# One batched attention and convolution kernel on one core: the v rows of its second pass loaded in two pieces that do not overlap

## The chip, the cores and the metric

The kernel runs on one core of a Trainium2 chip. The time is the device time of one launch in microseconds. Before the change it is 3721.15 us, the median of three runs (3717.85 to 3721.29). The profile is of one further execution, with a time of its own.

## The reference

The input x is a batch of 8 images of 256 channels and 64 x 64 pixels, in float32. Two layers follow each other. The first is an attention with keys and values from a 4 x 4 strided convolution. The second, which the change concerns, makes q, k and v by a 1 x 1 convolution, runs a depthwise 5 x 5 convolution over all three, mixes the result in groups of eight channels, and uses both the plain and the convolved set for a linear attention:

```python
qkv = jnp.einsum('oc,bchw->bohw', w_qkv, x)
dw = jax.lax.conv_general_dilated(qkv, w_dw, window_strides=(1, 1), padding=[(2, 2), (2, 2)], ...)
agg = jnp.einsum('goi,bgihw->bgohw', w_pw, dw.reshape(B, G, I, H, W)).reshape(B, G * O, H, W)
ms = jnp.concatenate([qkv, agg], axis=1)
...
kv = jnp.einsum('bhnd,bhne->bhde', k, v)
out = jnp.einsum('bhnd,bhde->bhne', q, kv)
out = out[..., :-1] / (out[..., -1:] + ATT_EPS)
```

Here n runs over the 4096 pixels, q and k are passed through a ReLU, and v has a column of ones added.

## The kernel before

The kernel has three passes, and keeps what one leaves for the next in scratch tensors in device memory. The first pass (`first_pass`) runs the first layer and the 1 x 1 convolution of the second. It writes q and k as planes (`planes`), k once more as tokens (`kd`), and v as tokens (`vd`). Image b has in `vd[b]` eight blocks, one for each 32 channels. A block is a grid of 34 x 34 tokens of 128 floats, 512 bytes each: a token holds a 2 x 2 cell of pixels with 32 channels, and the outermost tokens are a border of zeros (`border`).

The second pass (`second_pass`, from line 1121) makes the sums over pixels of k times v, for the plain and for the convolved set, and the convolved q. It works through 64 units, `(t, k, b)`: two halves of the channels, four blocks in each, eight images. For unit u it

- loads kq and vq (`load_tokens`, lines 1162 to 1176), the planes d1 and d0 that the convolutions of k and q need (`load_cells`, line 1158), and for each new (t, k) the convolution weights w (`load_weights`, line 1152);
- makes the differences c of neighbouring cells (`paired`, lines 1185 to 1189, on VectorE and GpSimd);
- convolves k on TensorE (`convolve`, line 1244), finishes it as s on VectorE (line 1260) and r on ScalarE (line 1262);
- sums plain k times v (`summed_raw`, line 1277), after a ReLU of kq on ScalarE (`positive`, line 1227);
- sums convolved k times v (`summed`, line 1294), a unit later. This uses that a convolution of v against k is a sum over shifted v: each partition needs its tokens and their neighbours;
- convolves q (line 1248, then s and r in lines 1260 and 1264), two units later, and stores it (`stored`, line 1343), with the small stores kv (line 1326) and kvg (line 1336).

For vq a partition has four rows of six tokens. The 128 partitions are 16 pairs of token rows times eight groups of four columns. A partition reads the two rows of its own and two further ones, and in each the four columns of its group and the two that follow, which are also the first two of the next group. The load is one transfer for each of the four rows, with a source that steps by four tokens and reads six: its rows of 3072 bytes overlap by 1024 (lines 1173 to 1175). vq has three buffers in turn, kq, d1 and d0 two each.

`summed_raw` reads rows 1 and 2 of vq and tokens 1 to 4; `summed` reads all of vq.

The third pass (`third_pass`) divides by the sums, projects, adds and writes the output. Its first loads and products (`ahead`) are called for in the last five units of the second pass: raw (line 1449, with a ReLU in line 1538), the sums kvp and kvq (lines 1491 and 1493), agg (line 1465).

All transfers are issued by SyncE, in one queue, in the order that the scheduler of the framework gives them; it orders each engine's instructions by its own estimates, save where `tc.keep_in_program_order` holds them. A transfer waits for its buffer to come free, and for its landing semaphore: there are eight, used in turn, so a transfer waits until the one eight before it has landed.

Of the kernel before, what the change touches and what calls it, by code (L numbers as in the profile page):

```python
# [32 lines left out]
P = 128  # L33
# [4 lines left out]
NB = HH // R  # L38
# [1082 lines left out]
def second_pass(ctx: ExitStack, tc: tile.TileContext, a, planes, kd, vd, wtd, kvd, kvg, qd, ahead):  # L1121
    nc = tc.nc
# [39 lines left out]
    def load_tokens(u):  # L1162
        t, k, b = units[u]
        kq = (odd if u % 2 else first).tile([P, 2, 4, P], F32, tag=f"kq_{u % 2}", name=f"kq_{u}")
        nc.sync.dma_start(
            kq.rearrange("p a c e -> p a (c e)"),
            kd[b][4 * t + k].rearrange("a y (m i) b e -> (y m) a (i b e)", i=2),
        )
        kqs[u] = kq
        vq = (first, odd, second)[u % 3].tile([P, 4, 6 * P], F32, tag=f"vq_{u % 3}", name=f"vq_{u}")  # L1170
        v = vd[b][4 * t + k]
        row = (NB2 + 2) * P
        for r in range(4):
            src = [[2 * row, NB], [4 * P, NB // 2], [1, 6 * P]]
            nc.sync.dma_start(vq[:, r], bass.AP(tensor=v.tensor, offset=v.offset + r * row, ap=src))
        vqs[u] = vq.rearrange("p r (c f h e) -> p r c f h e", c=6, f=4, h=4)


# [13 lines left out]
    for g in range(4):  # L1192
        load_weights(0, 1, g)
    load_cells(0, 1)
    load_tokens(0)
    load_cells(1, 1)
    load_tokens(1)
    def load(home, src, name):
        t = home.tile(list(src.shape), F32, tag=name, name=name)
# [150 lines left out]
    for u in range(n_all + 3):  # L1350
        p, q, r = u - 1, u - 2, u - 3
# [5 lines left out]
        if 1 < u < n_all - 1:  # L1357
            load_tokens(u + 1)
# [511 lines left out]
```

## Time and profile before

| | us |
|---|---|
| median of three runs | 3721.15 |
| the profiled execution | 3723.3 |
| its span, first to last instruction | 3721.5 |
| TensorE busy | 3655.3 |
| VectorE busy | 2050.1 |
| ScalarE busy | 1348.7 |
| GpSimd busy | 1362.7 |
| TensorE line 1244 (convolution of k) | 376.9 |
| TensorE line 1294 (sums over vq) | 308.6 |
| TensorE clock granted, share of full | 0.991 |

The page of the profile gives busy time, not useful time: matmuls are pipelined, and the record of a matmul can hold some waiting. The busy tenths cut the span in 40 slices of 93 us; the second pass fills those from about the 22nd to the 33rd. A transfer is listed by tile and source, with its kilobytes. The DMA share is the time that packets took, over that of 16 engines.

### The profile page before, as it was taken

The numbers are of one execution on the slowest core, as the hardware profiler recorded it, in microseconds if no ns is written. First come the engines' busy times: TensorE is split into PE (matmuls) and PEld (weight loads), VectorE is DVE, ScalarE is ACT, GpSimd is POOL, SyncE is SP. The second block draws the span as 40 slices with busy tenths as digits, with TensorE's granted clock in tenths as the row PEclk, the third lists the DMA queues.
The fourth block names the chain that finished last, engine by engine and source line by source line (L and its number), as shares of the span: only waits on it lengthen the run. The fifth ranks groups of instructions, "written<-read, shape, count | busy, mean of one in ns | idle before, by whom it ended". The sixth has DMA issues, their size and how long they took to land.

```text
span 3721.5 us, 65545 instructions
## 1 busy us (share of the span) xinstructions
PE 3655.3 (98%) x25506; PEld 2021.3 (54%) x25506; DVE 2050.1 (55%) x3159; ACT 1348.7 (36%) x2761; POOL 1362.7 (37%) x1394
## 2 busy tenths in 40 slices
PE   8999999999999999999998999999999999999998
PEld 4443534435334344353336888888888884333333
DVE  1567576675766755746675544444444445445442
ACT  2344354443443534434542222322222223333322
POOL 2434343343443433434443333433334321222222
PEclk9999999999999999999999999999999998999999
DMA  5336456464464553543648999999989968778773
GB/s 180 103 104 188 130 143 179 129 190 145 123 206 120 150 156 106 145 124 96 176 111 234 265 275 273 252 248 263 266 242 261 240 187 234 224 216 238 226 213 102
DMA packets 557071, 693.98 MB, mean 186 GB/s; under 512 B 79952, under 2 KB 416336, under 8 KB 556752
## 3 DMA queue, kind: packets, MB, share of 16 engines
q1 hardware_dynamic: 556752, 689.70, 66.2%
q8 instruction: 203, 3.33, 0.4%
q14 instruction: 116, 0.95, 0.1%
HBM read 415.15 MB, written 274.40 MB: 185 GB/s over the span
## 4 chain that ended last, share of the span: by engine, by line
PE 94%; DMA 2%; DVE 1%; ACT 1%; issue 1%; SPq 1%; POOL 0%; POOLq 0%; ACTq 0%; DVEq 0%
PE qkv L917 16%; PE p L1593 12%; PE cv L1244 9%; PE cv L1248 9%; PE sc L795 7%; PE sums L1294 7%; PE av L819 6%; PE o L873 6%; PE q L780 6%; PE sr L707 6%; PE den L839 3%; PE rep L1579 2%; PE den L1560 1%; PE raw L1277 1%; DMA wsr<-in_w_sr_dram 1%
## 5 line engine op out<-in xcount | busy, mean ns | idle before, releaser
L832 POOL TENSOR_TENSOR ej<-e,e 128x512 f32<-128x512 f32 x512 | 679.2, 1355 | 957.8 <-ACT e L801 957.8
L801 ACT ACTIVATE e<-sc 128x512 f32<-128x512 f32 x1024 | 529.9, 608 | 581.9 <-PE sc L795 581.9
L1244 PE MATMUL cv<-w,c 128*128 128x128 f32 x3072 | 376.9, 280 | 7.3 <-DVE eps L1615 6.2
L1260 DVE TENSOR_TENSOR s<-cv,both 128x512 f32<-128x512 f32 x256 | 176.6, 691 | 374.5 <-PE cv L1244 192.4
L1244 PEld LDWEIGHTS cv<-w,c 128*128 128x128 f32 x3072 | 354.8, 192 | 37.5 <-issue 36.4
L1603 POOL TENSOR_TENSOR y<-z,xs 128x512 f32<-128x512 f32 x128 | 165.7, 1302 | 458.6 <-ACT z L1601 427.0
L1294 PE MATMUL sums<-vq,r 128*32 128x288 f32 x4096 | 308.6, 414 | 0.2 <-issue 0.2
L795 PE MATMUL sc<-q,kk 32*128 32x512 f32 x2048 | 299.6, 639 | 0.0
L917 PE MATMUL qkv<-differences,combined 128*128 128x512 f32 x576 | 291.3, 597 | 0.5 <-POOL differences L890 0.5
L1593 PE MATMUL p<-raw,wp 128*128 128x512 f32 x512 | 246.9, 604 | 5.2 <-ACT z L1601 5.1
L819 PE MATMUL av<-e,vv 128*32 128x512 f32 x2048 | 248.3, 598 | 0.6 <-ACT e L801 0.6
L707 PE MATMUL sr<-x,wsr 128*128 128x256 f32 x1024 | 235.3, 384 | 9.1 <-DMA wsr<-in_w_sr_dram 9.1
L780 PE MATMUL q<-x,wq 128*128 128x512 f32 x512 | 241.9, 594 | 0.0
L1593 PE MATMUL p<-agg,wp 128*128 128x512 f32 x512 | 240.4, 592 | 0.0
L1248 PE MATMUL cv<-c,w 128*128 128x128 f32 x2048 | 239.1, 275 | 0.0
L1248 PEld LDWEIGHTS cv<-c,w 128*128 128x128 f32 x2048 | 234.3, 192 | 0.0
L873 PE MATMUL o<-att,wout 128*128 128x512 f32 x512 | 231.2, 593 | 0.0
L1251 ACT COPY both<-cv 128x512 f32<-128x512 f32 x128 | 74.9, 585 | 429.1 <-PE cv L1244 370.1
L707 PEld LDWEIGHTS sr<-x,wsr 128*128 128x128 f32 x1024 | 195.8, 192 | 63.8 <-issue 26.2
L852 DVE STREAM_TRANSPOSE rden<-den 128x512 f32<-128x512 f32 x128 | 90.9, 710 | 216.7 <-PE den L839 211.8
L788 ACT COPY q<-q 128x512 f32<-128x512 f32 x128 | 75.1, 586 | 371.7 <-PE q L780 371.7
L933 DVE TENSOR_TENSOR whole<-part,qkv 128x512 f32<-128x512 f32 x256 | 172.6, 684 | 67.2 <-ACT part L979 47.3
(143 smaller groups left out, 5277.2 us busy)
## 6 DMA issues: line engine op xcount, KB each, us to landing
vq<-v SPq DMA_DIRECT2D x256, 384.0 KB
planes<-stage SPq DMA_DIRECT2D x128, 578.0 KB
d<-planes SPq DMA_DIRECT2D x128, 578.0 KB
raw<-planes SPq DMA_DIRECT2D x64, 578.0 KB
x<-in_xp_dram SPq DMA_DIRECT2D x64, 512.0 KB
wsr<-in_w_sr_dram SPq DMA_DIRECT2D x128, 256.0 KB
x<-x SPq DMA_DIRECT2D x128, 256.0 KB
k<-turned SPq DMA_DIRECT2D x256, 128.0 KB
```

The source lines that it names most:

```text
L707: nc.tensor.matmul(ps[:, oc], w[:, ci, oc * P : (oc + 1) * P], strips(b, f // 2)[:, ci, f % 2 * NK : (f % 2 + 1) * NK], start=(f == ci == ...
L780: nc.tensor.matmul(ps, consts["wq"][:, ci, c * P : (c + 1) * P], strips(b, s)[:, ci], start=(ci == 0), stop=(ci == 1),)
L795: nc.tensor.matmul(scs[h], kks[b][rows, c, kc * P : (kc + 1) * P], qs[rows], start=True, stop=True)
L801: nc.scalar.activation(e, scs[h], AF.Exp, scale=D0**-0.5)
L819: nc.tensor.matmul(sums["av"][cols], vvs[b][:, kc, c * P + h * D0 : c * P + (h + 1) * D0], es[h], start=(kc == 0), stop=(kc == 1),)
L832: nc.gpsimd.tensor_tensor(e, es0[h], es1[h], ALU.add)
L873: nc.tensor.matmul(ps, consts["wout"][:, c, oc * P : (oc + 1) * P], att[c], start=(c == 0), stop=(c == 1))
L917: nc.tensor.matmul(ps, w, x, start=True, stop=True)
L1244: nc.tensor.matmul(out, x, m, start=(da == 0), stop=(da == 1))
L1248: nc.tensor.matmul(out, m, x, start=(da == 0), stop=(da == 1))
L1294: nc.tensor.matmul(ps[h * D0 : (h + 1) * D0, : 36 * D1].rearrange("p (r n e) -> p r n e", r=3, e=D1), kt[:, par, h, 2 * r + c], vq[:, r : ...
L1593: nc.tensor.matmul(as_block(ps, i // 2), wp[:, i, oc * P : (oc + 1) * P], block(g, i // 2, i % 2, j), start=(i == 0), stop=(i == 3),)
```

## The change

Each of the four rows of vq is loaded by two transfers instead of one: the four tokens of the partition's own group (2048 bytes), and the two tokens that follow (1024 bytes), into the same places of the same tile. First come the four rows' own tokens, then the four rows' two further ones. A unit so has eight vq transfers instead of four, of 256 and 128 KB instead of 384; the bytes that are read stay the same. No transfer names an address twice.

```diff
         row = (NB2 + 2) * P
-        for r in range(4):
-            src = [[2 * row, NB], [4 * P, NB // 2], [1, 6 * P]]
-            nc.sync.dma_start(vq[:, r], bass.AP(tensor=v.tensor, offset=v.offset + r * row, ap=src))
+        own = 4 * P
+        for c0, n in ((0, own), (own, 2 * P)):
+            for r in range(4):
+                src = [[2 * row, NB], [own, NB // 2], [1, n]]
+                nc.sync.dma_start(
+                    vq[:, r, c0 : c0 + n], bass.AP(tensor=v.tensor, offset=v.offset + r * row + c0, ap=src)
+                )
         vqs[u] = vq.rearrange("p r (c f h e) -> p r c f h e", c=6, f=4, h=4)
```

The scheduler then places some instructions of the second pass otherwise, in both ends of it: on VectorE the c of unit 6 comes after the s of unit 5 instead of before, on ScalarE the r of unit 55 before the second ReLU of raw, and on SyncE the second half of the first raw load after d, kv and kvg.

## The prediction

> **What bounds the kernel now.** I read the page first: its head, the busy tenths, the queues and the transfers.
>
> ```profile
> span 3721.5 us, 65545 instructions
> PE 3655.3 (98%) x25506; PEld 2021.3 (54%) x25506; DVE 2050.1 (55%) x3159; ACT 1348.7 (36%) x2761; POOL 1362.7 (37%) x1394
> PE   8999999999999999999998999999999999999998
> DMA  5336456464464553543648999999989968778773
> ...
> vq<-v SPq DMA_DIRECT2D x256, 384.0 KB
> ```
>
> TensorE is busy for 98%. All that it leaves idle is 3721.5 - 3655.3 = 66 us, and no cheaper transfer can bring more than the part of it that waits for transfers. But in the middle of the DMA row, where the second pass is, the engines stand at 9: nearly full. The changed transfer, vq, moves 256 x 384 KB, 1.57 MB in each of 64 units.
>
> Next I took windows. Columns: window, length, busy time of PE, PEld, DVE, ACT and POOL, TensorE clock, DMA share, GB/s.
>
> ```profile
> 2505.00:2506.00 1.00, 1.00 (x12) 1.00 (x11) 0.47 (x3) 0.10 (x1) 0.00 (x0) 1.00 0.65 236
> 2507.00:2512.00 5.00, 5.00 (x46) 5.00 (x45) 2.88 (x7) 1.38 (x3) 1.63 (x2) 1.00 1.05 242
> 2514.00:2515.00 1.00, 1.00 (x12) 1.00 (x11) 0.36 (x1) 0.60 (x2) 0.13 (x1) 1.00 1.00 391
> 2519.50:2522.00 2.50, 2.50 (x28) 1.93 (x21) 2.34 (x6) 0.00 (x0) 0.00 (x0) 1.00 0.53 142
> 2040.00:2240.00 200.00, 195.82 (x2683) 167.11 (x2683) 96.09 (x178) 54.96 (x81) 77.73 (x85) 0.99 1.01 270
> 2300.00:2900.00 600.00, 600.00 (x8298) 519.94 (x8297) 286.52 (x543) 172.50 (x254) 239.22 (x254) 1.00 0.93 255
> ```
>
> One packet's time is 16 engines x bytes x share / rate. The second window holds vq alone, in rows of 3072 bytes: 16 x 3072 x 1.05 / 242 = 213 ns. The third holds weight rows (w) of the same 3072 bytes: 126 ns. So vq is read at some 60% of the rate that the same row has elsewhere. The first window is kq, rows of 2048 bytes: 90 ns; the fourth is q, rows of 1024 bytes: 61 ns. The last two rows give the stage: at the start of the pass transfers are full (1.01) and TensorE misses 4.2 us of 200; from 2300 to 2900 they are at 0.93 and TensorE misses nothing.
>
> Who TensorE waits for, from 2000 to 2940 us:
>
> ```profile
> PE few L1330 <- POOL red_agg L1222: 4.0, 1, 4.0
> PE raw L1277 <- ACT kq L1227: 2.8, 1, 2.8
> PE cv L1244 <- issue: 1.1, 1, 1.1
> PE sums L1294 <- issue: 0.2, 1, 0.2
> ```
>
> The first is the ramp of the pass, with no transfer behind it. The second has one, seen on VectorE and ScalarE:
>
> ```profile
> 2110.63 0.73 DVE L1185 TENSOR_TENSOR c<-d 128x544 f32<-128x544 f32 x1 [5.72 <-DMA d<-planes]
> 2111.27 0.72 DVE L1186 TENSOR_TENSOR c<-d 128x544 f32<-128x544 f32 x1
> 2111.91 1.28 DVE L1260 TENSOR_TENSOR s<-cv,both 128x512 f32<-128x512 f32 x2
> ```
>
> VectorE waits 5.72 us for a d tile, with s queued behind it, and s leads over r to kq and to TensorE's raw. Last, SyncE's queue in one unit of the steady stage:
>
> ```profile
> 2503.48 0.54 SPq L1165 DMA_DIRECT2D kq<-k  x1
> 2504.12 2.48 SPq L1175 DMA_DIRECT2D vq<-v  x4
> 2509.64 0.81 SPq L1152 DMA_DIRECT2D w<-wt  x2
> 2511.82 0.37 SPq L1158 DMA_DIRECT2D d<-planes  x1
> ```
>
> Four vq issues take 2.48 us, 0.62 each, and 5.2 us pass between the last of them (2506.6) and the next d, which waits for TensorE to leave its buffer.
>
> [...] kq, vq, w and d follow each other in the windows as they were issued, so a slow vq delays the d behind it. [...] the trace's rows (90 ns for 2048 bytes, 61 for 1024, 126 for 3072) agree that cutting a row costs a little.
>
> **The change part by part.**
>
> *Bytes and packets.* The same 3072 bytes per partition and row now come as 2048 and 1024. Before, the two steady windows that I took of vq alone gave 213 ns and, at 2524 to 2529 us, 16 x 3072 x 0.99 / 253 = 192; I take 200. A unit has 4 x 128 rows on 16 engines, 32 per engine: 32 x 200 = 6.4 us. After, if overlap was the cause: 32 x (90 + 61) = 4.8 us; saved 1.6 us per unit. If it was not, and the time goes by bytes, 6.4 again. If each packet paid the surplus over the w row (200 - 126 = 74 ns) for itself, 32 x (90 + 74 + 61 + 74) = 9.6 us, 3.2 more. I take the first: kq also has neighbouring rows of neighbouring partitions, but touching and not overlapping, and is fast, and w has rows far apart and is fast. Overlap is what vq alone has. The ends -1.6 and +3.2 us per unit stay for the range.
>
> *Steady stage.* TensorE misses nothing there, so saved transfer time is worth nothing. What hides a loss: 0.93 of a 16.6 us unit is 15.4 us of transfers, 1.2 us free. A vq is also issued early: the one at 2504 us is for unit 33, used by raw at 2532.7 us, 29 us after its kq was issued (12 to 20 us in the first units); landed by about 2515, it has some 17 us in hand.
>
> *SyncE's queue.* Eight issues in place of four: + 4 x 0.62 = 2.5 us per unit, in front of w, d, kv, kvg and the q stores. The 5.2 us before d cover it: the last vq issue moves to 2509.1, w to 2510.3, d stays at 2511.8. The program gives its transfers eight landing semaphores in turn, each waiting for the transfer eight before; eight shorter transfers are fewer bytes in flight, but at 4.8 us of data against 5 us of issue the queue is not starved. Cost 0. In the first pass the two early loads (1834 to 1843 us) take 5 us more of a queue that stands idle until 1847.8 us: 0 to 0.3 us, on stores that nobody waits for there.
>
> *Order.* The scheduler moves things. VectorE gets s of unit 5 ahead of c of unit 6, the pair of the 2110 us stall: its 2.8 us go even if transfers stay slow. With vq 1.6 us shorter in each of the first units, the d loads come earlier, and the 1.1 and 0.2 us go too: -4.2 us. At the start of the third pass, ScalarE waits 4.92 us for the load of raw, and TensorE 3.53 us at 2951.75 us for the kq behind it. That load stands behind vq: the four more issues delay it 2.5 us (2940.65 to 2943.1), the faster vq leaves the engines free just then; two changes that cancel, 0 +- 1.5 us. The next stall (3.02 us at 3024) hangs on 14 small transfers after q, and those of 3092 on the new pass's loads; no vq stands in them: 0.
>
> *Sum.* The profiled execution took 3723.3 us, 1.8 us around its span. 3723.3 - 4.2 = 3719.1. The median of the runs (3721.15) lies 2.15 us under the profiled one, so the median after is 3717.0. A measurement of this kernel can tell about 0.2%, 7.4 us, from no change: this would not be told.
>
> **The rivals.**
>
> *Rates stay, only the order moves.* For it: no price is known for overlap, and vq's rate wanders (213 and 192 ns) as it would if the placing of v in memory slowed it. Then the start stays full; -2.8 us from the order, up to +3 from the longer queue: 3721.
>
> *Slower: each of the two packets pays the surplus.* In the steady stage transfers would need 15.4 + 3.2 = 18.6 us of 16.6, and become the bound. It decides from about 1.5 us more per unit (1.2 free, and 17 us in hand over some 57 units), that is vq above 7.9 us, 247 ns per row. Price: 57 x 2.0 - 17 = 97 us, 3818. Against it: kq and q rows show no such surplus. A part of it (a halo that is slow alone, +1.6 us) would still be just hidden or cost some 10 to 20 us, 3735.
>
> *Slower: SyncE too late.* If landing waits stretch the eight issues by more than the 2.7 us left before d, d, kv and q come late, then c, and TensorE at cv: up to 0.3 us in each of 57 units, 3738. Against it: from 2300 to 2900 the queue waits on a landed vq for 1.8 us in all.
>
> *Faster still.* The stall at 2951 us goes as well, as ScalarE's order there also changes (r before the second raw): another -3.5 us, 3713.5.
>
> **How the numbers follow.** Forecast 0.55; rates stay 0.17; faster still 0.11; full surplus 0.06; partial surplus or a late SyncE 0.11. The forecast's own range is 3713 to 3721. From 3710 to 3732 all but the full surplus, half of the partial cases and a small tail are held, some 0.85. Faster by over 0.2% (under 3713.7): half of the last rival and a tail of the forecast, 0.14. Slower (over 3728.6): 0.06 + 0.11 and 0.01, 0.18. Between: 0.68.
>
> **What would show it.** Right: packets of 2048 and 1024 bytes where vq is, at over 330 GB/s and some 130 to 150 ns for the pair; DMA share from 2300 to 2900 near 0.84; TensorE without the waits at 2111 and 2156 us, still 600 of 600 busy in the steady stage; SyncE's d still waiting for TensorE. Wrong: a share of 1.0 all through the pass and TensorE waits on kq, raw or c in every unit; or d issued later than TensorE frees it.

## The result and the profile after

The changed kernel takes 3716.43 us, the median of 20 runs (3712.05 to 3722.2); the kernel before, in 20 runs beside it, 3721.2 us (3714.88 to 3730.65). The ratio is 0.9985, 95% interval 0.9979 to 0.9992: 4.8 us less. The interval leaves out 1, so the gain is real, though smaller than the 0.2% that the forecast took as the least that a measurement could tell. The profiled execution took 3715.08 us with a span of 3713.3 us.

The head of the page of the changed kernel, its DMA tenths and one of its two vq rows:

```profile
span 3713.3 us, 65717 instructions
PE 3653.4 (98%) x25506; PEld 2021.5 (54%) x25506; DVE 2051.1 (55%) x3159; ACT 1349.4 (36%) x2761; POOL 1366.2 (37%) x1394
...
DMA  5336456464464553543648999889989868778773
...
vq<-v SPq DMA_DIRECT2D x256, 256.0 KB
```

TensorE's work is the same (3653.4 us against 3655.3); what it leaves idle went from 66 to 60 us. In the DMA tenths three nines became eights, and that is all.

Windows of the changed kernel (length, busy time of PE, PEld, DVE, ACT, POOL, TensorE clock, DMA share, GB/s). The first two hold vq, the third is the start of the second pass, the fourth its steady stage:

```profile
2504.00:2505.00 1.00, 1.00 (x11) 1.00 (x10) 0.24 (x1) 0.00 (x0) 0.00 (x0) 1.00 1.01 234
2506.50:2509.00 2.50, 2.50 (x23) 2.50 (x22) 1.87 (x4) 1.04 (x2) 1.80 (x2) 1.00 1.11 259
2040.00:2240.00 200.00, 198.17 (x2714) 171.11 (x2713) 98.94 (x183) 55.69 (x83) 78.72 (x85) 1.00 1.00 272
2300.00:2900.00 600.00, 600.00 (x8240) 519.97 (x8233) 290.78 (x544) 171.69 (x252) 240.13 (x252) 1.00 0.89 254
```

vq still comes at 234 to 259 GB/s, as before (242 and 253). The steady share fell from 0.93 to 0.89, not to 0.84. At the start transfers are still full (1.00), and yet TensorE misses 1.8 us of 200 there in place of 4.2.

TensorE's waits in the second pass, to 2940 us, after:

```profile
PE few L1334 <- POOL red_agg L1226: 4.0, 1, 4.0
PE raw L1281 <- ACT kq L1231: 1.3, 1, 1.3
PE cv L1248 <- issue: 0.5, 1, 0.5
```

The ramp (4.0) is as before; the three others, 4.1 us together, have become 1.8. VectorE near the place where it stood 5.72 us before, in order of time:

```profile
2109.37 0.69 DVE L1264 TENSOR_TENSOR s<-cv,both 128x512 f32<-128x512 f32 x1 [3.27 <-issue]
2111.10 0.69 DVE L1264 TENSOR_TENSOR s<-cv,both 128x512 f32<-128x512 f32 x1 [1.04 <-PE cv L1252]
2111.71 0.72 DVE L1189 TENSOR_TENSOR c<-d 128x544 f32<-128x544 f32 x1
2112.34 1.84 DVE L1190 TENSOR_TENSOR c<-d 128x544 f32<-128x544 f32 x1
```

The two s now stand ahead of c, and c no longer waits for d. This looks as if the order at this place had done it; the experiments say that this place alone did not. SyncE in one steady unit:

```profile
2500.01 0.53 SPq L1165 DMA_DIRECT2D kq<-k  x1
2500.63 5.04 SPq L1177 DMA_DIRECT2D vq<-v  x8
2506.34 0.81 SPq L1152 DMA_DIRECT2D w<-wt  x2
2508.53 0.37 SPq L1158 DMA_DIRECT2D d<-planes  x1
```

Eight vq issues take 5.04 us, 0.63 each. That d still waits for TensorE is in SyncE's waits from 2300 to 2900 us: the queue of d (L1158) waits 50.4 us in 36 times for TensorE, against 150.4 us in 36 times before, and 8.8 us for a landed vq. So 100 us over 36 units, 2.8 us each, of the slack in front of d have been used up, and none of it reached TensorE.

### Where the time went, by stage

The start of line 1277's products for a unit (raw of unit 0, 16, 56) gives the length of each stage in the two traces, in us:

| stage | before | after |
|---|---|---|
| raw of unit 0 to raw of unit 16 | 260.3 | 257.8 |
| raw of unit 16 to raw of unit 56 | 664.2 | 664.0 |
| raw of unit 56 to the last product of the sums | 145.3 | 142.9 |
| from there to the first product of the third pass's p | 41.7 | 38.9 |

Nothing in the steady stage, 2.5 us at its start, 5.2 us around the change to the third pass. The two traced executions lie 8.2 us apart (3723.3 and 3715.08 us), more than the medians do (4.8), so the table holds some scatter. The last two stages differ most from trace to trace (among the kernels with four transfers in the table at the end of the experiments their sum was 184.9 to 189.0 us), so the first row is the one that the experiments are about.

### The profile page after: what moved, and what is told of

Its sections match the earlier page's. It is cut to its first block, busy times and chain, and to the rows that moved or that the text cites. A ratio compares the mean times of both kernels' runs of the same rounds, so it can differ in the third digit from the quotient of the medians.

```text
span 3713.3 us, 65717 instructions
## 1 busy us (share of the span) xinstructions
PE 3653.4 (98%) x25506; PEld 2021.5 (54%) x25506; DVE 2051.1 (55%) x3159; ACT 1349.4 (36%) x2761; POOL 1366.2 (37%) x1394
## 4 chain that ended last, share of the span: by engine, by line
PE 93%; DMA 3%; DVE 1%; ACT 1%; issue 1%; SPq 0%; POOL 0%; POOLq 0%; ACTq 0%; DVEq 0%
PE qkv L917 16%; PE p L1597 12%; PE cv L1248 9%; PE cv L1252 9%; PE sc L795 7%; PE sums L1298 7%; PE av L819 6%; PE o L873 6%; PE q L780 6%; PE sr L707 6%; PE den L839 3%; PE rep L1583 2%; PE den L1564 1%; PE raw L1281 1%; DMA vq<-v 1%; DMA d<-planes 1%
```

## The experiments

Each was timed in five rounds beside the kernel before. The first four tell overlap, placing and the rest apart; the next two the order at one place; then the form of the access, that is, how many steps the source needs to get from partition to partition.

### v rows that do not overlap, in four transfers

The kernel before, with six tokens from one partition to the next in place of four. No transfer then names an address twice; different transfers still read common rows, as before. It reads other tokens of v than it should.

```diff
-            src = [[2 * row, NB], [4 * P, NB // 2], [1, 6 * P]]
-            nc.sync.dma_start(vq[:, r], bass.AP(tensor=v.tensor, offset=v.offset + r * row, ap=src))
+            src = [[2 * row, NB], [6 * P, NB // 2], [1, 6 * P]]
+            nc.sync.dma_start(vq[:, r], bass.AP(tensor=v.tensor, offset=v.offset + min(r, 2) * row, ap=src))
```

> The four transfers and the order of every engine of the kernel before, but the source steps by six tokens, so no address is read twice (the fourth row reads the third's place, and v is the wrong one: only the time counts). Overlap theory: a vq row of 3072 bytes falls from some 200 ns to about 126, the DMA share from 2300 to 2900 us from 0.93 to about 0.80, and the time to 3716 to 3718 with the order unchanged. Placing theory (rows are slow because of where 16 token rows lie in memory): 185 to 210 ns, share 0.92 to 0.94, 3721. Order theory (the gain is VectorE's s ahead of c, whatever the rate): the wait of some 2.8 us at 2110 us stays, 3721.

Measured: 3722.88 us (13 runs; the kernel before beside it 3721.57), ratio 1.0 (0.9992 to 1.0009). The two stages:

```profile
2040.00:2240.00 200.00, 195.87 (x2681) 168.54 (x2681) 92.34 (x178) 54.76 (x81) 74.32 (x85) 0.99 1.00 270
2300.00:2900.00 600.00, 600.00 (x8301) 519.98 (x8300) 286.25 (x542) 172.20 (x253) 238.02 (x254) 1.00 0.92 255
```

Start, share and rate are those of the kernel before (195.82 us, 0.93, 255 GB/s). Without overlap inside a transfer nothing is faster: this overlap is not what makes vq slow.

### The change, with the overlap put back

The changed kernel with its two kinds of transfer reading rows that overlap by a quarter and by a half. It reads other tokens of v than it should.

```diff
-                src = [[2 * row, NB], [own, NB // 2], [1, n]]
+                src = [[2 * row, NB], [3 * n // 4 if c0 == 0 else n // 2, NB // 2], [1, n]]
```

> The eight transfers and the order of every engine of the changed kernel, but the own four tokens step by three and the further two by one, so each transfer's rows overlap again (v is the wrong one: only the time counts). Overlap theory: the pair of packets rises from some 180 ns to 230 or more, the DMA share from 0.89 to 0.94 or more, and the time returns to 3720 or above. Placing theory: pair and share stay within 5% of the changed kernel's, 3716. Order theory: 3716 whatever the pair costs.

Measured: 3716.71 us (21 runs), ratio 0.9985 (0.9979 to 0.9992), to the digit that of the changed kernel. The gain stays with overlap and without. From both sides, then: the premise of the change is not the cause of its gain.

### Another place for v

Rows of v 64 tokens apart in memory in place of 34, once in the kernel before, once in the changed one. Both read the tokens that they should.

```diff
-        row = (NB2 + 2) * P
+        row = 64 * P
...
-    vd = [scratch(f"v_{b}", [8, NB2 + 2, NB2 + 2, P]) for b in range(B)]
+    vd = [scratch(f"v_{b}", [8, NB2 + 2, 64, P])[:, :, : NB2 + 2] for b in range(B)]
```

> The kernel before with the token rows of v in memory 64 tokens (32 KB) apart instead of 34 (17 KB); transfers, sizes, overlap and the order of every engine are those of before. Placing theory: vq rows at 120 to 140 ns, DMA share 0.80 to 0.84, 3716 to 3718. Overlap theory: rows stay at about 200 ns, share 0.93, 3721. Order theory: 3720 to 3721, the wait at 2110 us stays unless d comes earlier.

> The changed kernel with the token rows of v 64 tokens apart in memory. Placing theory: the pair of packets falls from some 180 ns to 130 to 150, share from 0.89 to 0.83, the last waits at the start of the pass (1.3 us for kq, 0.5 us for cv) go, 3714 to 3716. Overlap theory: nothing is left to gain from it, pair and share stay, 3716.

Measured: in the kernel before 3724.84 us (13 runs), ratio 1.001 (1.0002 to 1.0018); in the changed one 3716.71 us (12 runs), ratio 0.9982 (0.9974 to 0.9991). The placing brings nothing (in the kernel before it costs 0.1%). TensorE's waits of the first show how little the place of a stall means:

```profile
PE few L1330 <- POOL red_agg L1222: 4.0, 1, 4.0
PE sums L1294 <- issue: 2.6, 1, 2.6
PE raw L1277 <- ACT kq L1227: 2.5, 1, 2.5
```

The loss of 5 us at the start is there again, split over other products than before, with every engine's order unchanged.

### The order at one place, both ways

The forecast gave 2.8 us to VectorE's order: two s of unit 5 ahead of c of unit 6 (the c of q's convolution). Here the kernel before gets that order at that place, and the changed kernel loses it. Apart from TensorE's position of a few sums around raw of unit 8, that one swap is the only difference in each pair.

```diff
-        nc.vector.tensor_sub(v[:, 0], d0, d1)
-        nc.vector.tensor_sub(v[:, 1], d2, d1)
+        first_sub = nc.vector.tensor_sub(v[:, 0], d0, d1)
+        if what == 0 and u == 6:
+            behind(first_sub, put_s[5])
+        second_sub = nc.vector.tensor_sub(v[:, 1], d2, d1)
+        if what == 0 and u == 6:
+            behind(second_sub, put_s[5])
```

(`behind` holds an instruction behind another on the same engine; `put_s[5]` is the second s of unit 5.) In the changed kernel (`put_s[6, 0]` is the second subtraction of c of unit 6):

```diff
-        if conv:
+        if conv and q != 6:
             paired(q, 0)
+        if q == 5:
+            paired(6, 0)
...
-            nc.vector.tensor_add(s, ps, both)
+            put = nc.vector.tensor_add(s, ps, both)
+            if what == 0 and u == 5 and i == 0:
+                behind(put, put_s[6, 0])
```

> The kernel before with one thing moved: on VectorE the two subtractions of c of unit 6 (first convolution) stand behind the two additions s of unit 5, as they do in the changed kernel; four transfers of 3072-byte rows per unit stay, and SyncE's, ScalarE's and GpSimd's orders are those of before. Theory A (the order carries most of the gain, the transfers a smaller part): the wait of raw for ScalarE's kq (2.8 us near 2111 us) goes, the waits on issue (1.1 and 0.2) may stay; 3721.5 - 2.8 = 3718.7 us. Theory B (this one place of the order carries all of it): 3716.5, as after. Theory C (neither, the gain comes from fewer bytes in flight behind SyncE's landing slots): 3721.5, and the wait moves to another place nearby. Share of the transfers from 2300 to 2900 us 0.93 under all.

> The changed kernel with one thing moved back: c of unit 6 stands ahead of the two s of unit 5 on VectorE, as before; the eight transfers stay. d of unit 6 was issued at 2101.3 us in the changed kernel (2097.4 before) and is used at 2111.7 there without a wait. Theory A and B: c waits 4 to 5 us for d again, s behind it is late, TensorE's raw waits some 2.8 us for kq; A 3719.3 us (between the two kernels), B 3721. Theory C: 3716.5, c waits for d with nobody waiting behind, because the transfers land early enough. Share from 2300 to 2900 us 0.89 under all.

Measured: the kernel before with the new order 3720.77 us (13 runs; the kernel before beside it 3721.39), ratio 1.0 (0.9992 to 1.0008). The changed kernel with the old order 3714.68 us (13 runs), ratio 0.9977 (0.9969 to 0.9986). Theory A and B fall for this place: the swap brings no gain where it is put in, and none is lost where it is taken out. TensorE's waits to 2940 us in the first:

```profile
PE raw L1289 <- ACT kq L1237: 4.2, 2, 3.4
PE few L1342 <- POOL red_agg L1232: 4.0, 1, 4.0
```

The 2.8 us did go from their place, and 4.2 us stand elsewhere, as theory C had it (which doesn't show the cause that theory C named). VectorE in the second, at the old order:

```profile
2110.34 1.77 DVE L1195 TENSOR_TENSOR c<-d 128x544 f32<-128x544 f32 x1 [0.76 <-DMA d<-planes]
2112.04 1.25 DVE L1196 TENSOR_TENSOR c<-d 128x544 f32<-128x544 f32 x1
2113.21 0.68 DVE L1270 TENSOR_TENSOR s<-cv,both 128x512 f32<-128x512 f32 x1
```

c waits 0.76 us for d, not 5.72. With d there, it is of no account whether s stands before or behind.

The two runs test this place and no other. The account of the change names one place where VectorE's order differs; the traces show ten, nine of them from 2036 to 2204 us and one at 3034, and six on GpSimd from 2042 to 2194 us; SyncE's order differs at more places too, from 2197 us on. All kernels with eight transfers have the changed orders on VectorE and GpSimd, all with four have those of before, save for the one swap in this pair. One of the ten is where the 3.4 us of the first run's waits come from: there r on ScalarE waits for s, and kq and TensorE's raw come behind it. VectorE at that place, then in the changed kernel at the same unit:

```profile
2144.67 0.73 DVE L1191 TENSOR_TENSOR c<-d 128x544 f32<-128x544 f32 x1 [3.70 <-DMA d<-planes]
2145.31 0.72 DVE L1194 TENSOR_TENSOR c<-d 128x544 f32<-128x544 f32 x1
2145.95 0.68 DVE L1270 TENSOR_TENSOR s<-cv,both 128x512 f32<-128x512 f32 x1
...
2138.54 0.69 DVE L1264 TENSOR_TENSOR s<-cv,both 128x512 f32<-128x512 f32 x1 [1.09 <-PE cv L1248]
2139.15 0.15 DVE L1335 COPY m<-few 128x1 f32<-128x1 f32 x1
2140.86 0.98 DVE L1189 TENSOR_TENSOR c<-d 128x544 f32<-128x544 f32 x1 [1.56 <-DMA d<-planes]
```

In the first, s stands behind a c that waits 3.70 us for d; the changed kernel has it ahead. So what the order at the other places is worth to the changed kernel is not shown. What is left to test is whether an earlier d is enough with the order of before.

### One stride over the partitions

The overlap, the bytes, the number of transfers and every engine's order stay; only the source is one stride of four tokens over 128 partitions, in place of 16 token rows of eight groups. The partitions of the lower rows read other tokens than they should.

```diff
-            src = [[2 * row, NB], [4 * P, NB // 2], [1, 6 * P]]
+            src = [[4 * P, P], [1, 6 * P]]
```

> The kernel before with the source of vq as one stride of four tokens over 128 partitions (rows still overlap by two tokens, still 3072 bytes; the partitions of the lower image rows read other tokens of v than they should), in place of 16 image rows of eight. Order of every engine as before. Theory F (the two-level form of the access decides the rate, not overlap): the 3072-byte packets fall from 187 to about 126 ns, as in the weights' rows; 32 x 61 ns = 1.9 us less per unit of 16.6, so the share from 2300 to 2900 us falls from 0.93 to about 0.81. Theory G (overlap or the place of v matter, with the form nothing): 187 ns and 0.93. Time: with the order of before the stall of c at 2111 us shrinks as d lands earlier; if time follows transfers 3717, if it follows VectorE's order alone 3720 to 3722.

The same in the changed kernel (`[[own, P], [1, n]]`):

> The changed kernel with the sources of both kinds of transfer as one stride over 128 partitions (the partitions of the lower image rows read other tokens of v than they should). Order of every engine as after. Theory F: 2048-byte packets fall from 115 to about 90 ns and 1024-byte ones from 59 to about 50, the share from 2300 to 2900 us from 0.89 to 0.80 or less. Theory G: 115, 59 and 0.89. Time 3716.5 under both, since TensorE misses nothing in the steady stage and the order is that of after; if the rate carries time, some 2 us less.

Measured: 3714.6 us in four transfers (21 runs), ratio 0.9982 (0.9976 to 0.9989), and 3712.71 us in eight (9 runs), ratio 0.9977 (0.9967 to 0.9986). Windows of the first; the third line is vq alone:

```profile
2040.00:2240.00 200.00, 200.00 (x2745) 173.81 (x2745) 98.11 (x185) 57.86 (x86) 80.96 (x87) 1.00 0.82 272
2300.00:2900.00 600.00, 600.00 (x8229) 520.62 (x8229) 300.87 (x543) 172.60 (x254) 246.23 (x253) 1.00 0.81 254
2516.00:2519.00 3.00, 3.00 (x28) 3.00 (x27) 2.02 (x4) 0.93 (x2) 1.45 (x2) 1.00 1.02 364
```

vq alone now runs at 364 GB/s, 16 x 3072 x 1.02 / 364 = 138 ns per row in place of some 200; the share falls to 0.81 as theory F had it, and TensorE misses nothing at the start. Overlapping rows at nearly the rate of the weights' rows (391 GB/s): the form of the access is what was slow. And four transfers in before's order reach what the change reaches: once the rows are fast, no other order is needed. Whether the changed kernel, whose rows are still slow, owes a part of its gain to its own order, this does not say.

### Form, or how far apart the rows lie

One stride also brings the rows closer. So two more sources in the kernel before, both in two levels that cannot be merged into one: 16 groups of eight with nearly the addresses of the single stride, and 2 groups of 64. Both read other tokens than they should.

```diff
-            src = [[2 * row, NB], [4 * P, NB // 2], [1, 6 * P]]
+            src = [[33 * P, NB], [4 * P, NB // 2], [1, 6 * P]]                  # 16 groups
+            src = [[(4 * 64 + 1) * P, 2], [4 * P, 64], [1, 6 * P]]             # 2 groups
```

> The kernel before with the step between the 16 image rows of vq's source shortened from 68 tokens to 33 (two levels as before, the addresses almost those of one stride, which would be 32; rows overlap; the partitions read other tokens of v than they should). Order of every engine as before. Theory form (two levels in the access make vq slow): 3072-byte packets 185 ns as before, share from 2300 to 2900 us 0.93, 3721 us. Theory address (how far apart the rows lie): 131 ns, 0.81, 3714.6 us, as with one stride.

> The kernel before with vq's source as 2 groups of 64 rows (step of 4 tokens within a group, 257 tokens between the groups; two levels, not to be merged into one; the partitions read other tokens of v than they should). Order of every engine as before. If any second level is slow: 185 ns and 0.93, 3721 us. If short runs of eight rows are what is slow: about 131 ns and 0.81, 3714.6 us. In between: a share that says how the cost goes with the length of the run.

Measured, 16 groups: 3719.95 us (13 runs; the kernel before beside it 3720.56), ratio 0.9991 (0.9983 to 0.9999). Start, steady stage and vq alone:

```profile
2040.00:2240.00 200.00, 195.58 (x2673) 166.49 (x2672) 90.89 (x176) 55.20 (x81) 76.51 (x85) 0.98 0.99 271
2300.00:2900.00 600.00, 600.00 (x8244) 519.87 (x8245) 287.16 (x543) 173.51 (x255) 238.41 (x254) 1.00 0.91 256
2510.00:2512.00 2.00, 2.00 (x20) 2.00 (x20) 0.91 (x5) 0.63 (x1) 0.62 (x1) 1.00 1.01 237
```

16 x 3072 x 1.01 / 237 = 209 ns per row, and the start as before: 16 groups of eight are slow at nearly the same addresses. Theory form holds for these groups.

With 2 groups the kernel takes 5177.05 us (5 runs), ratio 1.391 (1.3889 to 1.3931). Neither of the two expectations named such a time. vq alone there:

```profile
3004.00:3008.00 4.00, 4.00 (x45) 2.83 (x38) 0.00 (x0) 0.07 (x1) 0.00 (x0) 0.93 0.14 56
3044.00:3048.00 4.00, 4.00 (x38) 3.67 (x33) 0.00 (x0) 0.58 (x1) 0.00 (x0) 1.00 0.13 50
3050.00:3055.00 5.00, 5.00 (x45) 5.00 (x44) 0.00 (x0) 0.00 (x0) 0.69 (x1) 1.00 0.13 50
```

A share of 0.13 is that of 2 busy engines of 16. 50 GB/s are then 25 for each, and a row takes 16 x 3072 x 0.13 / 50 = 128 ns, nearly as with one stride (138). So a second level did not slow a row in this run; but its share was that of two engines, against 1.01 with 16 groups, which may be why. In both runs the share is that of as many engines as the source has groups; what brings this about is not shown.

### One row of four; the first units alone

In the kernel before, the single stride for the first of the four transfers of each unit, and, in another kernel, for all four but only in units 0 to 11. What it is used for reads other tokens than it should.

```diff
             src = [[2 * row, NB], [4 * P, NB // 2], [1, 6 * P]]
+            if r == 0:        # in the other kernel: if u < 12:
+                src = [[4 * P, P], [1, 6 * P]]
```

> The kernel before, with the one-stride source for the first of the four transfers of each unit alone (its partitions read other tokens of v than they should). A vq row was about 197 ns in the kernel before (the weights' rows of the same size taken out), 129 with one stride, and 180 for the pair in the changed kernel; here (3 x 197 + 129) / 4 = 180: the changed kernel's rate with four transfers and before's order. Theory rate (delivery of d in the first units sets the time): 3716.5 us as the changed kernel, share from 2300 to 2900 us 0.90, VectorE's waits for d from 2040 to 2240 us 5 to 20 us in place of 31 to 40. Theory slots (eight smaller transfers behind eight landing semaphores let SyncE reach d earlier): 3721, since there are four.

> The kernel before, with the one-stride source for units 0 to 11 alone (they read other tokens of v than they should), the two-level source from unit 12. Theory start (only the first units of the pass, where transfers are full, are worth time): nearly all of the gain of the one-stride kernel, 3715 to 3716 us; TensorE 200.00 of 200 busy from 2040 to 2240 us, share from 2300 to 2900 us 0.93 with 600.00 of 600 busy. Theory all units: about 12 / 64 of 6.8 us, 3720.

Measured for one row: 3719.74 us (14 runs), ratio 0.9993 (0.9985 to 1.0002). Its stages:

```profile
2040.00:2240.00 200.00, 195.89 (x2698) 168.22 (x2697) 97.01 (x183) 55.47 (x82) 78.76 (x85) 1.00 0.99 272
2300.00:2900.00 600.00, 600.00 (x8298) 519.95 (x8297) 292.43 (x543) 172.58 (x254) 240.80 (x254) 1.00 0.89 255
```

The steady share is the changed kernel's 0.89, as intended, and yet the start is that of the kernel before: 4.1 us missed. This looks like the theory called slots. But the traces, side by side below, show that at the start of the pass, where it counts, the flat row had brought the packets' time down by less than eight transfers do; and the ratio's interval overlaps that of the changed kernel (0.9979 to 0.9992). The run does not tell the two theories apart.

Measured for the first units: 3715.98 us (21 runs), ratio 0.9992 (0.9985 to 0.9999). Its stages:

```profile
2040.00:2240.00 200.00, 199.82 (x2740) 173.19 (x2740) 93.99 (x185) 57.23 (x84) 77.89 (x88) 1.00 0.88 267
2300.00:2900.00 600.00, 600.00 (x8231) 520.46 (x8230) 285.68 (x543) 172.19 (x253) 237.87 (x252) 1.00 0.92 254
```

The start is mended by the first twelve units alone, and the steady stage at 0.92 costs nothing. The median agrees with theory start; the ratio's interval, 0.4 to 5.6 us less, holds what both theories forecast and does not tell them apart.

### All of them side by side

From the traces, in us. "Packets": the durations of all packets from 2040 to 2900 us, summed, on each of 16 engines. "d": when the last of the 512 packets of d0 of unit 6 had come (packets of 1156 bytes, counted in order), after the first raw of the pass. "Ahead": the durations of all packets from the first raw to that landing, summed, on each of 16 engines. "c waits": VectorE's waits of c for d, 2040 to 2240 us. "Start": first raw to raw of unit 16.

| kernel | packets | d | ahead | c waits | TensorE of 200 | start | median |
|---|---|---|---|---|---|---|---|
| before | 817 | 119.9 | 120.6 | 39.9 | 195.82 | 260.3 | 3721.2 |
| rows apart | 814 | 119.4 | 118.4 | 33.1 | 195.87 | 260.6 | 3722.9 |
| before, other place | 812 | 119.2 | 118.5 | 31.2 | 194.85 | 262.6 | 3724.8 |
| before, new order | 807 | 118.5 | 118.5 | 31.0 | 195.81 | 259.5 | 3720.8 |
| 16 near groups | 805 | 120.3 | 117.6 | 34.8 | 195.58 | 261.5 | 3720.0 |
| one row of four | 787 | 119.5 | 116.8 | 33.7 | 195.89 | 259.5 | 3719.7 |
| after | 796 | 117.6 | 116.4 | 19.7 | 198.17 | 257.8 | 3716.4 |
| after, overlap | 795 | 114.0 | 114.1 | 9.4 | 200.00 | 255.2 | 3716.7 |
| after, other place | 790 | 115.0 | 111.9 | 5.2 | 200.00 | 255.2 | 3716.7 |
| after, old order | 788 | 116.9 | 114.8 | 9.0 | 200.00 | 255.3 | 3714.7 |
| first 12 units flat | 782 | 104.6 | 95.0 | 15.9 | 199.82 | 253.8 | 3716.0 |
| one stride, four | 698 | 104.2 | 94.6 | 3.3 | 200.00 | 253.2 | 3714.6 |
| one stride, eight | 710 | 105.5 | 99.2 | 3.1 | 200.00 | 254.3 | 3712.7 |

The start goes with the landing of d, whatever brought it about. With d at 118 to 120 us TensorE misses 4 to 5 us of 200, at 117.6 it misses 1.8, and at 117 or sooner next to nothing. With the flat sources d comes some 10 us earlier still, which is worth only 1 to 2 us more.

And d lands when the packets ahead of it have passed. In the ten kernels of the table whose rows are slow from the first unit on, the engines are full until then ("ahead" is 97 to 101% of the time to the landing), SyncE's order, the number of vq transfers aside, is the same in the kernel before and the changed one up to 2197 us, and the bytes that passed are nearly the same in all thirteen, 32.3 to 32.9 MB. So it is mostly the packets' time that differs: 117.6 to 120.6 us in the five slow kernels with four transfers, 111.9 to 116.4 in the four with eight, 94.6 to 99.2 with flat sources. One row of four has 116.8, hardly less than the first five.

## Why the prediction was right, and where its reasons were not

The forecast of 3717.0 us stands 0.6 us from the median, within its range. Its sum was 4.2 us of waits at the start of the pass, and 4.1 of them became 1.8 in the changed kernel's own trace and 0 in three variants with its eight transfers. So the place and the size were right, the size in part by luck: the sum gave 2.8 us to an order that at that place gives nothing, rested on a saving per unit four times too large, and left out a gain at the start of the third pass. In the three variants a d only 3 to 6 us sooner than before went with no wait at all. Two steps that led there were wrong.

**"After, if overlap was the cause: 32 x (90 + 61) = 4.8 us; saved 1.6 us per unit."** It failed as a cause and as a size. In the two overlap runs overlap costs nothing that can be told. The packets of the five four-transfer kernels that kept the slow source in all rows sum to 811 us per engine on average, those of the four eight-transfer kernels with the slow source to 792; over 860 us / 16.6 us = 52 units that is 0.37 us saved per unit. The share of 0.84 and the 330 GB/s that were to show the step right were not there (0.89; 234 to 259). The argument was "overlap is what vq alone has": it is not. Among the loads compared (kq and w) vq is also the one whose source needs two strides for its partitions, and going to one stride is what took the slowness away, about 2 us per unit ((811 - 704) / 52).

**"Its 2.8 us go even if transfers stay slow."** Refuted for the pair that it names: with slow transfers and the new order there, 4.2 us of waits stand elsewhere, and with the old order and eight transfers nothing is lost. The stall was read as a place, c ahead of s, when it was a lateness: c waits for d in 13 places in the kernel before, 39.9 us in all, and with one place mended the late d held up TensorE at another. By the same error the rival "rates stay, only the order moves" had -2.8 from a pair that by itself gives nothing. What the nine other places of VectorE's order give, neither the prediction nor a run priced.

**"With vq shorter in each of the first units, the d loads come earlier, and the 1.1 and 0.2 us go too."** This mechanism works, and it carries the 2.8 us as well: with the order of before and four fast transfers TensorE misses nothing. In the changed kernel d lands sooner too (117.6 us against 119.9; 114.0 to 116.9 in the three variants), with a quarter of the expected saving per unit, as the engines are full from the start of the pass (packets take 116.4 of the 117.6 us) and every unit's saving adds to the next. That this alone ended the waits there is likely but not shown, since the orders changed with it.

**Steady stage 0.** Right: 664.2 and 664.0 us from unit 16 to unit 56, and 600.00 of 600 busy.

**SyncE's four more issues cost 0.** Right: 5.04 us for eight, and d still waits for TensorE. The four issues took 2.5 us of the 5.2 in front of d, as worked out.

**Start of the third pass 0 +- 1.5.** Not confirmed. The trace pair shows 5.2 us less from raw of unit 56 to the first p (187.0 to 181.8 us). All other kernels of the table with four transfers took 184.9 to 189.0 us there, 185.3 with all rows on one stride; the others with eight took 177.9 to 184.2, the 177.9 with one stride. So it goes with the eight transfers, or with the order that comes with them (ScalarE's at 2952 us among it), and not with vq's rate. No run tells these two apart; whether it is what the rival "faster still" named stays open.

**The slower rivals.** Refuted by the runs: no surplus per packet (796 us of packet time against 817), no late SyncE.

**What stays open.** How much of the changed kernel's gain is d landing sooner and how much the other order of VectorE and GpSimd: no run has eight slow transfers in before's order, or four in the changed one. And whether eight slow transfers land d sooner than four by their packets' time alone. That time speaks for it (some 4 us less ahead of d), and one row of four flat is no argument against it, since early in the pass it saved less than planned: from 2002 to 2108 us the 3072-byte packets, weights among them, took 175.8 ns, against 182.2 in the kernel before. The eight landing semaphores, which the 2467 transfers of SyncE in the trace before and the 2723 after use in turn, may have a part: from the issue of d0 of unit 6 to its last packet, 2.6 to 3.2 MB passed in the six kernels with four transfers in which all or most rows are slow, and 1.1 to 1.9 MB in the four with eight. But with four fast ones it is 1.4 to 1.5 MB as well. No run varies the number of transfers at one packet time, so this is argued and not shown.

## What to carry to other kernels

When one transfer runs below the rate of its neighbours, write down everything in which it differs from them before naming a cause, the number of strides that its partitions need among them, and vary one at a time. Where a stage is short of transfers, price an edit by when the late tile lands, not only by which instruction stands behind which in the trace: moving one waiter moved the wait (2.8 us went, 4.2 us stood elsewhere). Before an order is called tested, compare the whole order of every engine in the two kernels, not the place of the stall alone. And a saving per unit that is worthless in a steady stage that is covered can still pay at the start of the pass, where it adds up until the first tile is on time (here 0.2 us of 664 in the one, 2.5 us of 260 in the other).

## What the runs showed of the hardware

- Source rows that overlap inside a transfer showed no cost: 364 GB/s with 1024 of 3072 bytes overlapping (one stride), and with two strides 817 us of packet time per engine overlapping, 814 apart.
- A source in 16 groups of eight partitions was slow, one stride over the same 128 was not: 237 and 364 GB/s with all 16 engines busy (share 1.01 and 1.02), some 209 and 138 ns for a row of 3072 bytes.
- A source in 2 groups of 64 had a share of 0.13, that of two busy engines of 16: 50 GB/s, some 128 ns for a row, and 5177 us for the kernel. With 16 groups the share was 1.01. No run tells what brings this about.
- Why 16 groups are slower than one stride is not shown.
- A form of v that allows one stride (its last two tokens stored twice) was not tried. An estimate of what it could bring, from the one-stride runs (3714.6 and 3712.7 us): 2 to 4 us below the changed kernel's 3716.4. The intervals of the ratios overlap (0.9976 to 0.9989 and 0.9967 to 0.9986 against 0.9979 to 0.9992), so not even this much is told apart.
